# Nucleus search of a graph network's second step: the last threshold move takes its slope from the move before it, one estimate is made by one engine alone, and the sort has six rounds

## The chip, the core and the metric

The kernel runs on one core of a Trainium2 chip. A core has five engines that run their own instruction queues in order: PE (matrix multiply, with its weight loads shown as PEld), DVE (vector), ACT (scalar functions), POOL and SP; here SP only starts transfers. The metric is the time of one execution on the device in microseconds (us), as the median of several runs.

## The reference, cut to what matters

There are 4096 nodes with 256 features. A graph attention layer comes first and is not touched. The second layer does two steps of attention with a cut, each followed by a mix with the graph, and ends in a normalisation:

```python
def _top_p_attention(X, W1, W2, W3):
    q = X @ W1.T @ W2.T
    k = X @ W3.T
    probs = softmax(q @ k.T)                     # 4096 x 4096
    idx = argsort(-probs); sp = sorted probs; cs = cumsum(sp)
    keep_sorted = cs - sp < 0.9                  # the largest ones, up to 0.9 of the mass
    A = probs * mask
    return A / A.sum(-1)

R = (S + I) / row sums
for n in range(2):
    A = _top_p_attention(Xa, W1, W2, W3)
    Xf = R @ Xf
    Xa = A @ Xa
    Z = Z + Xf @ U1[n].T + Xa @ U2[n].T
h = X + Z, normalised, scaled and shifted; then added to x and normalised again
```

The costly part is to find, in each row of 4096 probabilities, the smallest one that is still kept.

## The kernel before, in words

The kernel has three stages: the graph attention up to about 930 us of the profiled span, step one of the nucleus layer to about 1800 us, step two from there to the end. The change concerns step two (`n == 1`).

**A tile.** A step works on 32 tiles of 128 rows (`RowTile`). A tile's 4096 logits come from PE in four pairs of 128x512 blocks (`logits`, L928), tile `lp`. The pool of `lp` has two buffers, so pair k+1 cannot start before ACT has copied pair k to `p` (`logits_evict`, L934). DVE finds the largest value (`top`, L945), ACT takes the exponentials (L952 and L963, two halves each). Then a threshold is found that lies a little above the cut:

- `scalars` and `scalars2` make the first threshold `t` from the row's spread.
- Three times (`estimate`, `join`, `move`; k = 0, 1, 2) the mass below `t` is summed and `t` is moved. For k = 0 DVE sums a quarter of the row (L1025, 128x1024). For k = 1 and 2 DVE sums one half of the row (128x2048) and ACT the other half by two passes, Relu and Sign (`estimate_half`, L1042 and L1045). `join` puts the halves together on DVE (L1060 to L1066), ACT takes a logarithm `y` (L1069), DVE makes the move `s` (L1077), ACT makes the new `t` (L1087) and the next goal (L1015).
- `lift` and `final`: DVE zeroes all values at or over `t` into `w` and sums the rest (128x4096).
- `tops`: the eight largest of each 128 of `w` (L938). `sort`: eight rounds of "largest eight, then strike them out" (L1117, L1119) give the 64 largest below `t`. `edge` and `inside` find in them where the cut lies; `cut` takes what is under it out of `p` (DVE L1177 strikes, POOL L1181 subtracts).
- `product`: PE transposes `p` (L1193), ACT copies the result (`at`, L1202), PE multiplies with the features (`ap`, L1211).

If a row's cut does not lie within the sorted values, a flag is set, and the whole layer is computed again by a general path at the end.

**Beside it.** The mix with the graph (`Mix`, tile `rp`, L1271) is 64 row blocks of PE work in both steps together, of which most fall into step two. Each of its eight parts (a "chunk": four blocks of rows, two matmuls each) is put between other PE work; after the last, ACT copies `rp` to `fx` (L1290), and `done` scales and splits it (DVE L1294, ACT L1296, L829, L830). From the middle of step two on, each finished block also goes through the output part (`place_out`: PE products `zp`, L1332, and two normalisations on DVE, ACT and POOL, L1343 to L1373).

**The order.** All four compute engines carry out what a plan says. Each part gets a time in units of one tile, tile i at i plus an offset of the table `T2` (L1388); the parts are sorted by these times, and the sorted order is the order of each engine's queue. The times set the order alone, not when something runs. The mixes of step two follow each other at `T2["mix"]`, 0.567 of a tile. Several tiles are under way at once: while tile i+1 gets its logits, tile i is at its last estimates and tile i-1 in its product.

In this text "p0" to "p3" are the ACT copies of the four pairs of logits, and "the sign block" is what ACT does for one half estimate: `t`, goal, Relu, Sign and two small copies of `t` (L1087, L1015, L1042, L1045, L1048, L1049). In the queue of ACT before the change, the sign block of tile i for k = 2 stands between p0 and p1 of tile i+1.

Of the kernel before, what the change touches and what calls it, by code (L numbers as in the profile page):

```python
# [16 lines left out]
AF = mybir.ActivationFunctionType  # L17
ALU = mybir.AluOpType
# [161 lines left out]
def graph_attention(  # L180
# [534 lines left out]

CHUNK = 128
TOP = 8
EST = (  # L720
    ((4.0, 0.8, 0.8), (8.0, 0.5, 1.2)),
    ((4.0, 1.0, 1.0), (8.0, 0.8, 0.8), (18.0, 0.5, 1.2)),
)
ROUNDS = (3, 8)
SUB = 4
START, SLOPE = 0.2, -2.65
ALONE = 0.04
SCALE = 2.0**11
TOL = 1e-5

# [2 lines left out]
def nucleus_layer(  # L733
# [5 lines left out]
    nc = tc.nc  # L739
    N = out.shape[0]  # L740
# [14 lines left out]
    for k, u in enumerate((U1T, U2T)):  # L755
        t = one.tile([P, STEPS, 2, D], F32, name=f"u{k}")
# [18 lines left out]
    def row(name, values):  # L775
        t = one.tile([P, len(values)], F32, name=name)
        for k, v in enumerate(values):
            nc.gpsimd.memset(t[:, k : k + 1], v)
        return t
# [2 lines left out]
    gains = [  # L782
        row(f"gains{n}", [down for _, down, _ in e] + [e[-1][2]]) for n, e in enumerate(EST)
    ]
    aims = [row(f"aims{n}", [aim for aim, _, _ in e]) for n, e in enumerate(EST)]

    xa = one.tile([P, NT, D + 1], F32, name="xa")
# [12 lines left out]
    junk_s = one.tile([P, N // 2], U8, name="junk_s")  # L800
    junk_v = one.tile([P, N // 2], U8, name="junk_v")
# [78 lines left out]
    class RowTile:  # L880
# [109 lines left out]
        def scalars2(self):  # L990
            q, z = self.q_row, all_z[:, self.at, :]
            self.gain = self.tiny("gain", len(self.est) + 1)
            nc.vector.tensor_scalar(self.gain, gains[self.n], q, None, ALU.mult)
            self.tau = self.tiny("tau")
            nc.vector.tensor_scalar(self.tau, q, SLOPE, START, ALU.mult, ALU.add)

            self.left = self.tiny("left")
            if self.n == 0:
                nc.vector.tensor_scalar(
                    self.left, self.z, TOP_P, self.zc, ALU.mult, ALU.subtract  # L1000
                )
                self.rest = self.tiny("rest")
                nc.vector.tensor_scalar(self.rest, self.zc, self.rz, -1.0, ALU.mult, ALU.mult)
                nc.vector.tensor_scalar(self.rest, self.rest, 1.0 + 1e-6, None, ALU.add)
            else:
                nc.vector.tensor_scalar(self.left, self.z, TOP_P - 1.0, None, ALU.mult)
                self.rest = small
                self.rzs = self.tiny("rzs")
                nc.vector.tensor_scalar(self.rzs, self.rz, float(SUB), None, ALU.mult)


        def set_goal(self, k):
# [14 lines left out]
            )  # L1027
            return b

        def halves(self, k):  # L1030

            return self.n and k

        def estimate_half(self, k):

            if self.halves(k):
                cols = self.p[:, N // 2 :]
                part = self.tiny("halves", 6)
                self.signs, self.gaps, self.t_half, self.t_all, self.m, self.both = (
                    part[:, i : i + 1] for i in range(6)  # L1040
                )
                nc.scalar.activation(  # L1042
                    junk_s, cols, AF.Relu, bias=self.t, scale=-1.0, accum_out=self.gaps
                )
                nc.scalar.activation(  # L1045
                    junk_s, cols, AF.Sign, bias=self.t, scale=-1.0, accum_out=self.signs
                )
                nc.scalar.activation(self.t_half, self.t, AF.Copy, scale=0.5)  # L1048
                nc.scalar.activation(self.t_all, self.t, AF.Copy, scale=float(N // 4))  # L1049

        def estimate(self, k):
            sub = SUB if self.n and k == 0 else 2 if self.halves(k) else 1
            b = self.under(junk_v, sub)
            self.b, self.sub = b, sub

        def join(self, k):
            b, sub = self.b, self.sub
            if self.halves(k):

                nc.vector.tensor_scalar(  # L1060
                    self.m, self.signs, self.t_half, self.t_all, ALU.mult, ALU.add
                )
                nc.vector.tensor_scalar(
                    self.m, self.m, self.gaps, 0.0, ALU.subtract, ALU.max
                )
                nc.vector.tensor_scalar(self.both, self.m, b, None, ALU.add)  # L1066
                b, sub = self.both, 1
            self.y = self.tiny("y")
            nc.scalar.activation(  # L1069
                self.y, b, AF.Ln, scale=self.rzs if sub > 1 else self.rz, bias=self.rest  # L1070
            )

        def move(self, k):

            last = k == len(self.est) - 1
            s = self.tiny("s")
            nc.vector.tensor_scalar(  # L1077
                s, self.y, self.goal, self.gain[:, k : k + 1], ALU.subtract, ALU.mult
            )
            if last:  # L1080
                s1, s = s, self.tiny("s2")
                nc.vector.tensor_scalar(
                    s, self.y, self.goal, self.gain[:, k + 1 : k + 2], ALU.subtract, ALU.mult
                )
                nc.vector.tensor_scalar(s, s, s1, None, ALU.min)
            self.t = self.tiny("t")
            nc.scalar.activation(self.t, s, AF.Exp, scale=-1.0, bias=self.tau)  # L1087
            if not last:
                tau = self.tiny("tau")
                nc.vector.tensor_scalar(tau, self.tau, s, None, ALU.subtract)  # L1090
                self.tau = tau
                self.set_goal(k + 1)

        def lift(self):

            f = self.tiny("f")
            nc.vector.tensor_scalar(f, self.t, self.rz, ALONE, ALU.mult, ALU.is_ge)
            t = self.tiny("tf")
            nc.vector.tensor_scalar(t, f, 10.0, self.t, ALU.mult, ALU.add)
            self.t = t  # L1100
# [277 lines left out]
    def at(time, part, *args):  # L1378
        plan.append((time, len(plan), part, args))
# [3 lines left out]
        tops=0.105, top=0.882, spread0=1.093, exp_cand=1.477, spread1=0.939, exp0=1.191,  # L1383
# [1 line left out]
        move1=1.853, lift=1.861, final=1.897, sort=1.983, edge=2.281, select=2.299, product=2.548,  # L1385
        lag=0.218, out=0.344, qt=0.253, q1=0.460, q2=0.612, space=0.125, apart=0.250, split=0.300,
    )
    T2 = dict(top=0.512, spread0=0.616, spread1=0.514, exp0=0.670, exp1=0.604, scalars=0.726, scalars2=0.793, est0=0.807, join0=0.813, move0=0.856, est1=0.884, join1=0.931, move1=1.062, est2=1.204, join2=1.220, move2=1.326, lift=1.522, final=1.619, tops=1.657, sort=1.824, edge=2.072, inside=2.085, cut=2.275, product=2.354, lag=0.090, out=0.060, qt=-0.078, q1=0.444, q2=0.541, space=0.067, apart=0.074, mix=0.567, copy=0.030)  # L1388

    def carry_out():  # L1390
        for _, _, part, args in sorted(plan, key=lambda e: e[:2]):
# [56 lines left out]
    def place_second(t, time):  # L1448

        place_queries(t, time - 1, T2)  # L1450
        for k in range(4):
            at(time + k * T2["apart"] + 0.01, t.logits, k)
            at(time + k * T2["apart"] + T2["copy"], t.logits_evict, k)
        at(time + T2["top"], t.top)
        for k in range(2):
            at(time + T2[f"spread{k}"], t.spread, k)
            at(time + T2[f"exp{k}"], t.exp, k)
        at(time + T2["scalars"], t.scalars)
        at(time + T2["scalars2"], t.scalars2)
        for k in range(len(EST[1])):  # L1460
            if k:
                at(time + T2[f"move{k - 1}"] + 0.002, t.estimate_half, k)
            at(time + T2[f"est{k}"], t.estimate, k)
            at(time + T2[f"join{k}"], t.join, k)
            at(time + T2[f"move{k}"], t.move, k)
        at(time + T2["lift"], t.lift)
        at(time + T2["final"], t.final)
        for b in range(8):
            at(time + T2["tops"], t.tops, w, b)
        for k in range(ROUNDS[1]):  # L1470
            at(time + T2["sort"] + 0.018 * k, t.sort, k)
        at(time + T2["edge"], t.edge)
        at(time + T2["inside"], t.inside)
        for k in range(4):
            at(time + T2["cut"] + 0.04 * k, t.cut, k)
        place_product(t, time + T2["product"], T2)

    def place_out(m, time):
        at(time + 0.03, m.out_load)
        at(time - 0.3, m.out_load_f)  # L1480
        at(time + 0.3, m.out_load_x)
        for k in range(4):
            at(time + 0.01 + 0.09 * k, m.out_transpose, k)
            at(time + 0.06 + 0.09 * k, m.out_product, k)
        at(time + 0.36, m.out_sum)
        at(time + 0.50, m.out_norm)
        at(time + 0.70, m.out_stats)
        at(time + 0.80, m.out_store)

# [3 lines left out]
    with tc.manual_schedule(  # L1495
# [16 lines left out]
        time = 0.0  # L1512
# [6 lines left out]
        for i, m in enumerate(mixes[1]):  # L1519
            time = max(time, i + 3.4)  # L1520
# [423 lines left out]
```

## Time and profile before

| | |
|---|---|
| median of 3 runs | 3541.23 us (3536.95 to 3541.74) |
| the profiled execution | 3550.11 us, of it 3548.3 us span |
| busy in the span | PE 91%, DVE 83%, ACT 71%, PEld 58%, POOL 17% |
| graph attention, 0 to 930 us | PE 820.5, DVE 802.7, ACT 739.7 us busy |
| step one, 930 to 1800 us | PE 848.3, DVE 634.8, ACT 654.0 us busy |
| step two, 1800 to 3549 us | PE 1556.8, DVE 1521.0, ACT 1120.1 us busy |

The tiles of step two begin (DVE L945) at 1867.0 us for the first and 3393.3 us for the last. The table of stages that the profile gives has one row per stretch of time, with each engine's busy time in it, the granted clock of PE as a share of full speed, and the DMA traffic. A view of waits says which instruction of an engine stood idle for whom, with the total, the number of times and the longest.

### The profile page before, as it was taken

To read this page: it belongs to the slowest core of one execution; us is meant where nothing else is said; L and a number is where in the kernel's file an instruction comes from. 1 tells how busy PE (TensorE), PEld (TensorE's weight loads), DVE (VectorE), ACT (ScalarE), POOL (GpSimd) and SP (SyncE) were. 2 spreads that over 40 slices of the span, in tenths; PEclk is the share of its full clock that TensorE was granted. 3 is DMA by queue.
4 is the path that set the end of the run, shared out by engine and by line. 5 is a ranking of instruction groups with operands and counts; after the bars stand their busy time and mean duration, and the time that the engine had idled before them with its cause. 6 is when DMAs were issued, how large, how long until landed. Compare 5 with 4: busy or idle time off the path is not lost. (4 is left out here: it accounts for less than half of the span.)

```text
span 3548.3 us, 56062 instructions
## 1 busy us (share of the span) xinstructions
PE 3225.7 (91%) x19538; PEld 2074.7 (58%) x19538; DVE 2958.4 (83%) x8775; ACT 2513.8 (71%) x3938; POOL 601.7 (17%) x433
## 2 busy tenths in 40 slices
PE   8998889888789999999997899999899989999987
PEld 4522222222357777777874667666667767767765
DVE  4779989999568888888516999999989999999993
ACT  4678889889578888888516776677667667667652
POOL 1101450000000000000000222222222332322331
PEclk9999999999899999999998999999899999999998
DMA  9846543232332222222235444444544444444433
GB/s 211 133 112 143 128 125 129 104 111 87 96 123 104 81 102 104 104 82 102 92 120 151 118 119 112 116 116 118 160 108 107 106 114 108 106 112 106 111 79 79
DMA packets 637302, 402.60 MB, mean 113 GB/s; under 512 B 262672, under 2 KB 588304, under 8 KB 633936
## 3 DMA queue, kind: packets, MB, share of 16 engines
q1 hardware_dynamic: 626640, 315.03, 31.3%
q10 hardware_dynamic: 1536, 67.11, 5.2%
q0 software_dynamic: 8832, 16.78, 5.1%
q8 instruction: 155, 2.54, 0.3%
q14 instruction: 139, 1.14, 0.1%
HBM read 406.03 MB, written 118.62 MB: 148 GB/s over the span
## 5 line engine op out<-in xcount | busy, mean ns | idle before, releaser
L1271 PE MATMUL rp<-low,adj 128*128 128x258 f32 x1856 | 561.2, 392 | 30.4 <-ACT fx L1290 17.7
L1271 PE MATMUL rp<-p,short 128*128 128x256 f16 x1856 | 501.4, 297 | 0.3 <-DMA short<-adj_d 0.2
L604 DVE COPY_PREDICATED other<-mask,e 128x2048 f32<-128x2048 uint8 x176 | 451.6, 2575 | 53.6 <-ACT other L589 48.1
L1211 PE MATMUL ap<-xf,at 128*128 128x257 f32 x2048 | 495.4, 387 | 0.0
L1211 PE MATMUL ap<-xa,at 128*128 128x257 f32 x2048 | 487.5, 381 | 4.0 <-ACT at L1202 3.9
L1271 PEld LDWEIGHTS rp<-low,adj 128*128 128x128 f32 x1856 | 391.6, 211 | 139.8 <-issue 84.1
L1211 PEld LDWEIGHTS ap<-xf,at 128*128 128x128 f32 x2048 | 372.4, 190 | 133.2 <-ACT t L1087 22.7
L928 PE MATMUL lp<-kT,q 64*128 64x512 f32 x1024 | 349.6, 713 | 110.5 <-ACT p L934 109.9
L634 PE MATMUL acc<-other,v 128*32 128x512 f32 x2816 | 344.7, 608 | 76.9 <-DVE other L604 65.1
L582 ACT ACTIVATE e<-src,minus_flat,factors 128x2048 f32<-128x2048 f32 x176 | 367.9, 2090 | 64.9 <-DVE other L604 31.8
L1202 ACT COPY at<-tpa 128x512 f32<-128x512 f32 x448 | 261.1, 584 | 208.5 <-PE tpa L1193 206.7
L1211 PEld LDWEIGHTS ap<-xa,at 128*128 128x128 f32 x2048 | 372.4, 191 | 49.4 <-ACT at L1202 5.8
L589 ACT ACTIVATE other<-away,minus_flat 128x2048 f32<-128x2048 f32 x176 | 350.6, 1992 | 8.0 <-PE acc L634 6.2
L1181 POOL TENSOR_TENSOR p<-p,w 128x1024 f32<-128x1024 f32 x128 | 299.8, 2365 | 312.8 <-DVE w L1177 271.5
L934 ACT COPY p<-lp 128x512 f32<-128x512 f32 x512 | 273.0, 584 | 93.3 <-PE lp L928 93.0
L1193 PE MATMUL tpa<-ident,p 128*128 128x128 f32 x2048 | 311.2, 275 | 2.2 <-POOL p L1181 2.2
L952 ACT ACTIVATE junk_s<-p,htop 128x2048 uint8<-128x2048 f32 x128 | 255.7, 1997 | 40.7 <-DVE htop L947 40.4
L1193 PEld LDWEIGHTS tpa<-ident,p 128*128 128x128 f32 x2048 | 246.0, 141 | 40.3 <-issue 3.3
L1177 DVE MATCH_REPLACE8 w<-c,w 128x128 f32<-128x128 f32 x1024 | 268.0, 276 | 0.0
L634 PEld LDWEIGHTS acc<-other,v 128*32 128x32 f32 x2816 | 81.1, 111 | 304.8 <-DVE other L604 152.8
L963 ACT ACTIVATE p<-p,ntop 128x2048 f32<-128x2048 f32 x128 | 257.8, 2014 | 0.1
L938 DVE MAX8 c<-p 128x8 f32<-128x128 f32 x1024 | 209.6, 277 | 55.0 <-ACT p L934 51.8
(259 smaller groups left out, 5451.1 us busy)
## 6 DMA issues: line engine op xcount, KB each, us to landing
adj<-adj_d SPq DMA_DIRECT2D x464, 256.0 KB
mask<-adj_d SPq DMA_DIRECT2D x164, 256.0 KB
short<-adj_d SPq DMA_DIRECT2D x232, 128.0 KB
mask<-mask_d SPq DMA_DIRECT2D x60, 256.0 KB
adj<-in_adjT SPq DMA_DIRECT2D x48, 256.0 KB
mask<-in_adjT POOLq DMA_DIRECT2D x32, 256.0 KB, 8.1
adj_d<-mask SPq DMA_DIRECT2D x32, 256.0 KB
src<-src_d SPq DMA_DIRECT2D x8, 1024.0 KB
```

Source lines behind the costliest of these rows:

```text
L582: nc.scalar.activation(self.e, self.head.src, AF.Relu, scale=self.factor(0), bias=self.factor(2))
L589: nc.scalar.activation(self.other, self.head.away, AF.Identity, bias=self.factor(2))
L604: nc.vector.copy_predicated(self.other, self.mask, self.e)
L634: nc.tensor.matmul(head.acc[k][at : at + 32, :], weights, self.e[:, b * 512 : (b + 1) * 512], tile_position=(0, at), **ends,)
L928: nc.tensor.matmul(lp, self.q[rows, :], kT[rows, at], start=True, stop=True)
L934: nc.scalar.copy(self.p[:, b * 512 : (b + 1) * 512], lp)
L1177: nc.vector.match_replace(w[:, cols], self.cand[:, c * TOP : (c + 1) * TOP], w[:, cols], 0.0)
L1181: nc.gpsimd.tensor_tensor(self.p[:, cols], self.p[:, cols], w[:, cols], ALU.subtract)
L1193: nc.tensor.transpose(tp[:, q * P : (q + 1) * P], self.p[:, (b * 4 + q) * P : (b * 4 + q + 1) * P], ident,)
L1202: nc.scalar.copy(at, tp)
L1211: nc.tensor.matmul(self.ap[:, : D + 1], at[:, q * P : (q + 1) * P], self.cur[:, j, :], start=j == 0, stop=j == NT - 1,)
L1271: nc.tensor.matmul(self.rp[:, : part.shape[1]], a, part, start=start and k == 0, stop=stop and k == len(parts) - 1,)
```

## The change

Four things change in step two, and nothing in the other stages:

1. For k = 1 DVE no longer sums its half; the half that ACT sums stands for the row (scaled by 2). For k = 2 both halves are summed as before, and ACT takes two logarithms: one of its own half, one of the whole.
2. The last move divides the step of the second move by what it changed in ACT's half, within the bounds 0.48 and 0.64, in place of two fixed factors. That is seven small DVE instructions for three. The aims of the three estimates become 16, 16, 16 (they were 4, 8, 18), and the bound at which `lift` gives up a threshold 0.025 (0.04).
3. The sort has six rounds, 48 values.
4. The table `T2` has new offsets, the mix 0.576, and three output parts stand earlier.

```diff
-    ((4.0, 1.0, 1.0), (8.0, 0.8, 0.8), (18.0, 0.5, 1.2)),
+    ((16.0, 0.9, 0.9), (16.0, 0.9, 0.9), (16.0, 0.48, 0.64)),
-ROUNDS = (3, 8)
+ROUNDS = (3, 6)
-ALONE = 0.04
+ALONE = (0.04, 0.025)
...
         def estimate(self, k):
-            sub = SUB if self.n and k == 0 else 2 if self.halves(k) else 1
-            b = self.under(junk_v, sub)
+            self.b = self.under(junk_v, (4, None, 2)[k] if self.n else 1)
...
         def join(self, k):
+            if self.n and k:
                 nc.vector.tensor_scalar(
                     self.m, self.signs, self.t_half, self.t_all, ALU.mult, ALU.add
...
+                self.y_before, self.y_half = self.y, self.log_of(self.m, 1)
+                if k == 1:
+                    self.y = self.y_half
+                    return
                 nc.vector.tensor_scalar(self.both, self.m, b, None, ALU.add)
...
         def move(self, k):
+            if last and self.n:
+                nc.vector.tensor_scalar(less, self.y_before, self.y_half, 1.0 / CAREFUL[0], ALU.subtract, ALU.mult)
+                nc.vector.tensor_scalar(square, less, less, 1e-12, ALU.mult, ALU.add)
+                nc.vector.reciprocal(square, square)
+                nc.vector.tensor_scalar(more, self.moved, less, square, ALU.mult, ALU.mult)
+                nc.vector.tensor_scalar(more, more, gain, self.gain[:, k + 1 : k + 2], ALU.max, ALU.min)
+                nc.vector.tensor_scalar(error, self.y, self.goal, more, ALU.subtract, ALU.mult)
+                nc.vector.tensor_scalar(s, error, CAREFUL[1] / CAREFUL[0], error, ALU.mult, ALU.min)
...
-    T2 = dict(top=0.512, ... est1=0.884, join1=0.931, move1=1.062, est2=1.204, join2=1.220, move2=1.326, lift=1.522, ... sort=1.824, edge=2.072, inside=2.085, cut=2.275, product=2.354, ... mix=0.567, copy=0.030)
+    T2 = dict(top=0.481, ... join1=0.945, move1=1.068, est2=1.200, join2=1.232, move2=1.395, lift=1.497, ... sort=1.827, edge=2.032, inside=2.121, cut=2.230, product=2.354, ... mix=0.576, copy=0.042)
...
-        at(time + 0.50, m.out_norm)
-        at(time + 0.70, m.out_stats)
-        at(time + 0.80, m.out_store)
+        at(time + 0.46, m.out_norm)
+        at(time + 0.62, m.out_stats)
+        at(time + 0.70, m.out_store)
```

More of the change, by code (lines that the diff above doesn't have):

```diff
@@ L721 @@
     ((4.0, 0.8, 0.8), (8.0, 0.5, 1.2)),
-    ((4.0, 1.0, 1.0), (8.0, 0.8, 0.8), (18.0, 0.5, 1.2)),
+    ((16.0, 0.9, 0.9), (16.0, 0.9, 0.9), (16.0, 0.48, 0.64)),
 )
-ROUNDS = (3, 8)
-SUB = 4
+CAREFUL = (0.8, 1.2)
+ROUNDS = (3, 6)
+SHARES = (4.0, 2.0)
 START, SLOPE = 0.2, -2.65
-ALONE = 0.04
+ALONE = (0.04, 0.025)
 SCALE = 2.0**11
@@ L784, in nucleus_layer @@
     ]
+    shares = row("shares", SHARES)
     aims = [row(f"aims{n}", [aim for aim, _, _ in e]) for n, e in enumerate(EST)]
@@ L1007, in scalars2 @@
                 self.rest = small
-                self.rzs = self.tiny("rzs")
-                nc.vector.tensor_scalar(self.rzs, self.rz, float(SUB), None, ALU.mult)
+                self.rzs = self.tiny("rzs", 2)
+                nc.vector.tensor_scalar(self.rzs, shares, self.rz, None, ALU.mult)
         def set_goal(self, k):
@@ L1028, in under, with estimate_half, log_of @@
             return b
[L1030 to L1049, printed above, removed]
-        def estimate(self, k):
-            sub = SUB if self.n and k == 0 else 2 if self.halves(k) else 1
-            b = self.under(junk_v, sub)
-            self.b, self.sub = b, sub
+        def estimate_half(self):
+            cols = self.p[:, N // 2 :]
+            part = self.tiny("halves", 6)
+            self.signs, self.gaps, self.t_half, self.t_all, self.m, self.both = (
+                part[:, i : i + 1] for i in range(6)
+            )
+            nc.scalar.activation(
+                junk_s, cols, AF.Relu, bias=self.t, scale=-1.0, accum_out=self.gaps
+            )
+            nc.scalar.activation(
+                junk_s, cols, AF.Sign, bias=self.t, scale=-1.0, accum_out=self.signs
+            )
+            nc.scalar.activation(self.t_half, self.t, AF.Copy, scale=0.5)
+            nc.scalar.activation(self.t_all, self.t, AF.Copy, scale=float(N // 4))
+        def estimate(self, k):
+            self.b = self.under(junk_v, (4, None, 2)[k] if self.n else 1)
+        def log_of(self, b, share=None):
+            y = self.tiny("y")
+            scale = self.rz if share is None else self.rzs[:, share : share + 1]
+            nc.scalar.activation(y, b, AF.Ln, scale=scale, bias=self.rest)
+            return y
         def join(self, k):
-            b, sub = self.b, self.sub
-            if self.halves(k):
+            b, share = self.b, 0 if self.n and k == 0 else None
+            if self.n and k:
                 nc.vector.tensor_scalar(
@@ L1065, in join @@
                 )
+                self.y_before, self.y_half = self.y, self.log_of(self.m, 1)
+                if k == 1:
+                    self.y = self.y_half
+                    return
                 nc.vector.tensor_scalar(self.both, self.m, b, None, ALU.add)
[L1067 to L1071, printed above, removed]
+                b = self.both
@@ L1073, in move @@
+            self.y = self.log_of(b, share)
         def move(self, k):
             last = k == len(self.est) - 1
+            gain = self.gain[:, k : k + 1]
             s = self.tiny("s")
[L1077 to L1081, printed above, removed]
+            if last and self.n:
+                part = self.tiny("slope", 4)
+                less, square, more, error = (part[:, i : i + 1] for i in range(4))
@@ L1082, in move @@
                 nc.vector.tensor_scalar(
-                    s, self.y, self.goal, self.gain[:, k + 1 : k + 2], ALU.subtract, ALU.mult
+                    less, self.y_before, self.y_half, 1.0 / CAREFUL[0], ALU.subtract, ALU.mult
                 )
-                nc.vector.tensor_scalar(s, s, s1, None, ALU.min)
+                nc.vector.tensor_scalar(square, less, less, 1e-12, ALU.mult, ALU.add)
+                nc.vector.reciprocal(square, square)
+                nc.vector.tensor_scalar(more, self.moved, less, square, ALU.mult, ALU.mult)
@@ new lines, in move @@
+                nc.vector.tensor_scalar(
+                    more, more, gain, self.gain[:, k + 1 : k + 2], ALU.max, ALU.min
+                )
+                nc.vector.tensor_scalar(
+                    error, self.y, self.goal, more, ALU.subtract, ALU.mult
+                )
+                nc.vector.tensor_scalar(
+                    s, error, CAREFUL[1] / CAREFUL[0], error, ALU.mult, ALU.min
+                )
+            else:
+                nc.vector.tensor_scalar(s, self.y, self.goal, gain, ALU.subtract, ALU.mult)
+                self.moved = s
+                if last:
+                    s1, s = s, self.tiny("s2")
+                    nc.vector.tensor_scalar(
+                        s, self.y, self.goal, self.gain[:, k + 1 : k + 2], ALU.subtract, ALU.mult
+                    )
+                    nc.vector.tensor_scalar(s, s, s1, None, ALU.min)
@@ L1096, in lift @@
             f = self.tiny("f")
-            nc.vector.tensor_scalar(f, self.t, self.rz, ALONE, ALU.mult, ALU.is_ge)
+            nc.vector.tensor_scalar(f, self.t, self.rz, ALONE[self.n], ALU.mult, ALU.is_ge)
             t = self.tiny("tf")
@@ L1387, in nucleus_layer @@
     )
-    T2 = dict(top=0.512, spread0=0.616, spread1=0.514, exp0=0.670, exp1=0.604, scalars=0.726, scalars2=0.793, est0=0.807, join0=0.813, move0=0.856, est1=0.884, join1=0.931, move1=1.062, est2=1.204, join2=1.220, move2=1.326, lift=1.522, final=1.619, tops=1.657, sort=1.824, edge=2.072, inside=2.085, cut=2.275, product=2.354, lag=0.090, out=0.060, qt=-0.078, q1=0.444, q2=0.541, space=0.067, apart=0.074, mix=0.567, copy=0.030)
+    T2 = dict(top=0.481, spread0=0.650, spread1=0.518, exp0=0.653, exp1=0.593, scalars=0.728, scalars2=0.769, est0=0.800, join0=0.820, move0=0.835, join1=0.945, move1=1.068, est2=1.200, join2=1.232, move2=1.395, lift=1.497, final=1.643, tops=1.647, sort=1.827, edge=2.032, inside=2.121, cut=2.230, product=2.354, lag=0.090, out=0.060, qt=-0.077, q1=0.461, q2=0.489, space=0.067, apart=0.074, mix=0.576, copy=0.042)
     def carry_out():
@@ L1461, in place_second @@
             if k:
-                at(time + T2[f"move{k - 1}"] + 0.002, t.estimate_half, k)
-            at(time + T2[f"est{k}"], t.estimate, k)
+                at(time + T2[f"move{k - 1}"] + 0.002, t.estimate_half)
+            if k != 1:
+                at(time + T2[f"est{k}"], t.estimate, k)
             at(time + T2[f"join{k}"], t.join, k)
```

## The prediction

> **What bounds the kernel now.** The page comes first, then the table of stages for step two alone, since nothing else changes. One stretch has only mixes beside the search (11 tiles), the other has the output part too (13 tiles):
>
> ```profile
> core 0: us, PE busy (x) PEld busy (x) DVE busy (x) ACT busy (x) POOL busy (x), PEclk, DMA share, GB/s
> 2001.10:2508.90 507.80, 465.23 (x2602) 345.95 (x2603) 482.25 (x1859) 356.33 (x651) 124.69 (x75) 0.93 0.46 117
> 2661.00:3344.60 683.60, 630.19 (x3625) 484.28 (x3624) 643.56 (x2494) 470.70 (x952) 201.89 (x134) 0.97 0.43 109
> ```
>
> A tile takes 46.2 us in the first stretch and 52.6 us in the second. DVE is busy 95% and 94% of it, PE 92% in both. DVE looks like the bound. The waits of 2000 to 2500 us, by engine, say whether it is the only one:
>
> ```profile
> PE lp L928 <- ACT p L934: 34.9, 16, 4.3
> PE rp L1271 <- ACT fx L1290: 7.4, 5, 4.0
> ```
>
> ```profile
> DVE all_z L977 <- ACT p L963: 7.8, 5, 2.6
> DVE halves L1060 <- ACT halves L1049: 2.9, 3, 1.6
> DVE s L1077 <- ACT y L1069: 0.7, 1, 0.7
> ```
>
> DVE's named waits are 11.4 us in eleven tiles, 1.0 a tile; about 1.3 us more are unnamed gaps between its some 170 instructions a tile. PE's waits are 42.3 us, nearly all its idle time in that stretch (507.8 less 465.2). So PE stands still only for ACT's copies, 3.8 us a tile. The order of time shows where (PE and ACT, one tile):
>
> ```profile
> 2167.51 1.13 PE L928 MATMUL lp<-kT,q 64*128 64x512 f32 x4
> 2170.25 1.61 PE L928 MATMUL lp<-kT,q 64*128 64x512 f32 x4 [0.44 <-ACT p L934]
> 2176.12 1.79 PE L928 MATMUL lp<-kT,q 64*128 64x512 f32 x4 [3.08 <-ACT p L934]
> ```
>
> ```profile
> 2169.64 1.05 ACT L934 COPY p<-lp 128x512 f32<-128x512 f32 x2
> 2170.58 0.30 ACT L1087 ACTIVATE t<-s,tau 128x1 f32<-128x1 f32 x1
> 2173.32 2.00 ACT L1045 ACTIVATE junk_s<-p,t 128x2048 uint8<-128x2048 f32 x1
> 2175.51 1.04 ACT L934 COPY p<-lp 128x512 f32<-128x512 f32 x2
> ```
>
> PE finishes pair 0, ACT copies it (p0), then ACT runs the whole sign block (2170.58 to 2175.51, 4.9 us) before p1, and pair 2 waits for p1's buffer. PE has only two mix chunks and pair 1 to put into that time, some 3.3 us. Hence a stall of 3 to 4 us in nearly each tile. Its price is larger than itself:
>
> ```profile
> 2168.40:2175.88 7.48, 4.20 (x22) 2.40 (x20) 7.10 (x23) 7.41 (x15) 0.67 (x1) 1.00 0.80 206
> 2175.88:2184.00 8.12, 7.88 (x25) 4.26 (x25) 8.02 (x58) 3.39 (x8) 4.67 (x2) 0.59 0.23 50
> ```
>
> After the stall PE runs at a granted clock of 0.59 over 8.1 us, that is, some 6.8 us at half speed, 3.4 us of PE work lost.
>
> So there are two loops of nearly the same length. **PE's loop:** from the end of pair 0 to the start of pair 2, 7.95 us in the mean of tiles 3 to 14 (6.54 the shortest); from there to the end of the next tile's pair 0, 37.97 us, nearly without a wait. Sum 45.9 us. **DVE's loop:** 43.8 us busy, 1.3 of gaps, 1.0 of waits: 46.1 us. The change shortens the second by much and the first by little.
>
> **The change part by part.** The rows, from 2300 to 3100 us (16 tiles):
>
> ```profile
> L1025 DVE SCALAR_TENSOR_TENSOR junk_v<-p,t 128x2048 uint8<-128x2048 f32 x32 | 75.0, 2344 | 2.4 <-ACT t L1087 2.4
> L1117 DVE MAX8 s<-left 128x8 f32<-128x256 f32 x111 | 47.0, 423 | 1.0
> L1119 DVE MATCH_REPLACE8 left<-s,left 128x256 f32<-128x256 f32 x96 | 39.3, 409 | 0.0
> L1077 DVE TENSOR_SCALAR s<-y,goal,gain 128x1 f32<-128x1 f32 x48 | 12.7, 264 | 0.8 <-ACT y L1069 0.6
> ```
>
> *DVE, per tile.* The half sum of k = 1 goes: 2.34 and 0.08 for its accumulator. Its joining addition (L1066, 0.21) goes. Two rounds of sorting go, each 0.42 + 0.41 + 0.09 for the load of the values: 1.85. `edge` works on 48 in place of 64: its scan takes 0.28 at 64 and 0.92 at 256 wide, 3.3 ns an element, 0.05 for 16; four others at some 1 ns, 0.07; together 0.12. The last move loses 0.26 + 0.26 + 0.21 = 0.74 and gains seven instructions that the trace does not have: by nearest rows (0.21 with one column as operand, 0.26 with two, 0.15 a reciprocal), 3 x 0.21 + 3 x 0.26 + 0.15 = 1.56; between 1.1 (all at 0.15) and 1.9. Net 2.34 + 0.08 + 0.21 + 1.85 + 0.12 + 0.74 - 1.56 = 3.8 us a tile, 121 us over 32.
>
> *ACT, per tile.* One more logarithm, 0.39 (L1069). It stands between p2 and p3, where in the trace ACT has time: it is idle 30% in these stretches. Nothing on the path; if uncovered, 12 us in all.
>
> *A new wait.* Between the move of k = 0 and its join, DVE had tau (0.21), four rounds (3.7) and the half sum (2.43): 6.3 us, over ACT's 4.9 for the sign block and its start. In the changed order it has tau, four rounds and one more MAX8: 0.21 + 3.70 + 0.42 = 4.3 us. DVE will wait 0.8 us or more at L1060, more where ACT waits for PE ahead of the block (in one tile 1.31 us for `tpa`). Behind it in DVE's queue stand the edge, the cut and the next tile's maximum. Bounds 0.5 and 2.5, I take 1.1. DVE's loop becomes 43.8 - 3.8 + 1.3 + 1.0 + 1.1 = 43.4 us.
>
> *PE's loop.* The order of PE and ACT around the stall stays: p0, sign block, p1, and one chunk between pairs. What goes is lateness: p0 came 0 to 1.7 us after pair 0 was ready (2168.64 to 2169.64 above), because ACT was behind DVE, whose maximum started 2 to 3 us after p3 was done. With DVE ahead, I put pair 0 to pair 2 at 6.9 us, near the shortest. The mix costs PE 19.1 us each (515.5 us for 27 in the same window); at 0.576 a tile holds 1.736 of them, not 1.764: 0.5 us less. 6.9 + 37.97 - 0.5 = 44.4 us. PE's loop is then the longer one.
>
> A rule speaks for more. The Trainium skill, "Perfetto Trace Analysis", section Identifying the Most-Contended Engine, says the engine with the highest occupancy is the one to optimise first; that is DVE, and taken alone it would pay out all 121 us, less the new wait. The waits of PE speak against it: 92% busy, and all of the rest tied to ACT in a loop of 45.9 us. I follow the loop. Another rule bears on the stall: "TensorE: Matmul & The Clock Gate", section HAM oscillation, warns of idle gaps over some 3.4 us. The trace has half speed after 3.08 already. My 6.9 less 3.3 leaves 3.6 us, so the half speed stays; if the stall fell clear of it, another 3.4 us a tile would come.
>
> *Output part.* In most tiles with outputs a scaling of `h` (L1354, 0.60) stood in ACT's queue between p0 and the block; with the earlier offsets it is gone from there. The earlier store also gives the single buffer of `h` more time: DVE waited 13.6 us in all for `out_y`. Pair 0 to pair 2 was 8.5 us here, the rest 44.3. I take 1.2 off the first (0.6 and lateness) and 0.5 off the second: 1.7 a tile. POOL's work is unchanged in amount, and moved away from its subtractions.
>
> *The end.* The longer mix step pushes 27 x 0.5 = 14 us of PE work behind tile 28, where PE had room (81.7 of 98.4 us busy at 3344 to 3443). It is hidden there, but then PE is full and DVE's saving in the last two tiles, 6 us, shrinks to 2. The last tile alone gains two rounds less what the new last move costs: 1.5.
>
> *Sum:* tiles 3 to 15, 13 x 1.6 = 21; tiles 16 to 29, 14 x 1.7 = 24; tiles 1 and 2, where p0 waits up to 7 us for DVE, 2 x 3 = 6; the last two, 2; the end, 1.5. Together 54 us. The profiled execution of 3550.1 us would become 3496; it lies 9 us over the median, and the same 54 us below the median give 3487. Differences under 0.2%, 7 us, could not be told from none.
>
> **The rivals.**
>
> *DVE's saving comes through (chance 0.15).* If lateness sits in all of PE's loop and the stall also drops under the half-speed point, tiles follow DVE's 43.4: 2.7 a tile, 85 us, and up to 120 without the new wait. For it: DVE's 95%. Against: PE's named waits.
>
> *The waits eat most (0.12).* If the join wait is 2.5 us and PE's loop keeps its lateness, 7 to 30 us remain.
>
> *Slower (0.07): the join of k = 1.* The place is L1060 behind the sign block; its price is whatever ACT's queue puts in front. DVE now has 4.3 us of cover. At a wait of more than 3.8 us the tile is longer than before, and each further us costs 32. That needs ACT to start the block 3 us late, as when `at` waits for `tpa` on PE; 1.31 us was seen, so it is unlikely. At 5 us: 38 us slower.
>
> *A missed row (0.03).* Only 48 values are sorted. I worked the new threshold rule through on the reference's inputs in float32: the farthest cut is the 45th value under the threshold. It is not far from 48[...]. One missed row adds the graph attention again (930 us) and a general search, milliseconds.
>
> **How the numbers follow.** The likeliest case, 30 to 80 us off, has 0.60, with 54 its middle: 3487. Full pass-through 0.15, small gain 0.12, no change 0.03, slower 0.10. The range leaves out the top of the full gain (over 100 us) and gains under 16 with what is slower: 3440 to 3525. Faster 0.87, same 0.03, slower 0.10.
>
> **What would show it.** DVE busy in step two falls by some 120 us, from 1521. A new wait of DVE at the join for ACT's `halves`, some 30 us in all. PE's wait for `p` stays at 3 us a tile and half speed stays after it; PE becomes the busiest, at 95% or more, DVE under 92%. Tiles at 44.4 and 50.9 us. If the stall of PE disappears, or tiles fall under 43.5, my loop was wrong; if DVE stays at 95%, the wait or the added instructions were mis-sized.

## The result and the profile after

The changed kernel takes 3508.70 us (median of 6 runs, 3506.38 to 3513.61), the kernel before in the same session 3539.38 us (6 runs, 3532.73 to 3545.73). The ratio is 0.9916, with a 95% interval of 0.9902 to 0.9930: 31 us faster, where 54 had been forecast; that lies at the lower edge of the likeliest case, 30 to 80. Line numbers of step two differ from those before by up to 23; the names, such as `lp` or `halves`, are the same.

The table of stages of the profile after, for the same 11 and 13 tiles as in the prediction, and then from tile 30 to the end:

```profile
1995.90:2492.50 496.60, 456.95 (x2594) 341.34 (x2594) 449.16 (x1802) 359.34 (x660) 120.74 (x75) 0.93 0.47 118
2632.40:3299.60 667.20, 629.48 (x3601) 483.51 (x3599) 604.06 (x2428) 476.00 (x964) 220.90 (x134) 0.96 0.44 111
3299.60:3505.50 205.90, 173.01 (x968) 138.26 (x966) 137.51 (x575) 95.72 (x203) 52.93 (x40) 0.90 0.37 94
```

A tile takes 45.1 us without outputs (46.2 before) and 51.3 with them (52.6). DVE, the third engine of the row after PE and PEld, fell from 95% to 90% busy; PE stayed at 92% in the first stretch and went from 92% to 94% in the second. The clock is 0.93 and 0.96, as good as unchanged. The waits of PE and of DVE in the first stretch:

```profile
PE lp L931 <- ACT p L937: 32.6, 11, 4.3
PE rp L1294 <- ACT fx L1313: 6.5, 5, 3.9
```

```profile
DVE halves L1062 <- ACT halves L1047: 16.8, 11, 2.6
DVE all_z L980 <- ACT p L966: 6.4, 8, 2.3
```

PE's wait for `p` is as it was (it was 34.9 us in 500), and DVE has the new wait at the join of k = 1, 1.5 us in each of eleven tiles. The order of time of one tile shows the reason (PE, then ACT; rows between are left out):

```profile
2204.31 1.13 PE L931 MATMUL lp<-kT,q 64*128 64x512 f32 x4
2212.69 1.96 PE L931 MATMUL lp<-kT,q 64*128 64x512 f32 x3 [3.60 <-ACT p L937]
```

```profile
2205.53 1.06 ACT L937 COPY p<-lp 128x512 f32<-128x512 f32 x2
2207.16 0.30 ACT L1110 ACTIVATE t<-s,tau 128x1 f32<-128x1 f32 x1
2212.08 1.05 ACT L937 COPY p<-lp 128x512 f32<-128x512 f32 x2
```

Pair 0 ends at 2205.44, and p0 starts 0.09 us later. In the mean of tiles 3 to 14 p0 was 1.1 us late before and is 0.25 us late now. The block (2207.16 to 2212.08, 4.9 us) and the stall of 3.6 us stand as they were. The chain that ended last, by engine, before and after (shares of the span; both chains reach back only over the last third of it):

```profile
DVE 12%; PE 11%; ACT 4%; issue 2%; DMA 1%; POOL 0%; SPq 0%; POOLq 0%; DVEq 0%; ACTq 0%
```

```profile
PE 18%; ACT 4%; DVE 4%; issue 2%; POOL 0%; DMA 0%; POOLq 0%; DVEq 0%; ACTq 0%
```

In this last third DVE's part fell from 12% to 4% of the span, and PE's rose from 11% to 18%.

From the starts of the tiles in both traces, the profiled executions (3550.11 and 3507.40 us) differ so: up to tile 3, 5 us less; tiles 3 to 15, 19 less; tiles 16 to 29, 21 less; from tile 30 to the end of the span, 2.5 more (205.9 against 203.4).

### The profile page after: what moved, and what is told of

Its sections match the earlier page's. It is cut to its first block, busy times and chain, and to the rows that moved or that the text cites. A ratio compares the mean times of both kernels' runs of the same rounds, so it can differ in the third digit from the quotient of the medians.

```text
span 3505.5 us, 55976 instructions
## 1 busy us (share of the span) xinstructions
PE 3219.6 (92%) x19538; PEld 2073.3 (59%) x19538; DVE 2862.1 (82%) x8615; ACT 2526.9 (72%) x3970; POOL 610.9 (17%) x435
```

## The experiments

Each kernel was timed beside the kernel before on the same chip. "Faster" and "slower" in us below compare medians of different sessions. The kernel before had medians of 3539 to 3548 us in these sessions, so such differences are good to some 9 us; the ratios carry their intervals, 5 to 9 us to either side.

| run | ratio to the kernel before | interval |
|---|---|---|
| the change | 0.9916 | 0.9902 to 0.9930 |
| 1, changed, eight rounds again | 0.9916 | 0.9897 to 0.9935 |
| 2, changed, DVE's half sum again | 0.9894 | 0.9876 to 0.9912 |
| 3, changed, mix spacing of before | 0.9919 | 0.9901 to 0.9937 |
| 4, changed, logits later | 0.9923 | 0.9908 to 0.9939 |
| 5, before, new order | 1.0032 | 1.0018 to 1.0045 |
| 6, changed, old order | 0.9956 | 0.9939 to 0.9973 |
| 7, changed, Sign pass twice | 1.0119 | 1.0099 to 1.0138 |
| 8, changed, half the mix | 0.9720 | 0.9700 to 0.9741 |
| 9, changed, block split | 0.9754 | 0.9737 to 0.9771 |
| 10, changed, block shorter | 0.9811 | 0.9792 to 0.9830 |
| 11, changed, split and shorter | 0.9768 | 0.9745 to 0.9790 |
| 12, before, block split | 0.9925 | 0.9904 to 0.9947 |

**Does DVE's saved work matter?** Two runs put parts of it back, with the rest of the change in place.

```diff
-ROUNDS = (3, 6)
+ROUNDS = (3, 8)
```

> The changed kernel with eight rounds of sorting again: DVE works 1.85 + 0.1 us more in each of 32 tiles, 62 us in all, and nothing else is different. Theory (PE's loop through ACT's sign block sets the tile, DVE has slack): DVE's tile was 40.8 busy of 44.9 us, with 1.5 us of it a wait at the join, so most of the 1.95 us fits into slack: 0 to 12 us slower than the changed kernel, about 3508 to 3521. Rival (DVE is the bound, as its 91 to 94% busy says): 50 to 62 us slower, 3560 or more, worse than the kernel before.

```diff
-            self.b = self.under(junk_v, (4, None, 2)[k] if self.n else 1)
+            b = self.under(junk_v, (4, 2, 2)[k] if self.n else 1)
+            if not (self.n and k == 1):
+                self.b = b
...
-            if k != 1:
-                at(time + T2[f"est{k}"], t.estimate, k)
+            at(time + (T2[f"est{k}"] if k != 1 else 0.900), t.estimate, k)
```

> The changed kernel with DVE's half sum for k = 1 done again, its result unused: 2.43 us of DVE work a tile, 78 us in all, put between the move of k = 0 and the join where DVE waits for ACT's sign block (16.8 us in some eleven tiles, 1.5 a tile). Theory: 1.5 us of it go into the wait and the rest into DVE's slack: 0 to 20 us slower than the changed kernel. Rival (DVE is the bound): 30 to 78 us slower, 30 if only the wait is filled.

Eight rounds: 3515.61 us, ratio 0.9916 as with the change. The half sum done again: 3502.63 us, and no slower either. DVE was busy 54 us longer in the one and 66 in the other (2915.6 and 2927.6 against 2862.1 us in the whole run), and neither cost anything that can be told from the spread. In the second run DVE's wait at the join went from 16.8 us (in 480) to 0.8:

```profile
DVE halves L1064 <- ACT halves L1047: 0.8, 2, 0.4
```

The wait was part of the room into which the work fitted. DVE alone as the bound is refuted. That the second run is a little below the change (0.9894 against 0.9916) is within the overlap of the intervals.

**The mix's spacing.**

```diff
-... mix=0.576, copy=0.042)
+... mix=0.567, copy=0.042)
```

> The changed kernel with the mixes 0.567 of a tile apart as before. Theory: each of some 27 tiles has 0.5 us more PE work (13 us), and the end, where PE did 13.5 us more than before and took 4 us more instead of 3 less, becomes shorter by 5 to 13 us: between 5 us faster and 8 us slower, no clear difference. Rival (PE's work in the tiles is not on the path): faster by the whole of the end, 5 to 13 us.

3514.51 us, no difference. In its trace, tile 30 to the end takes 202.1 us, against 205.9 with 0.576, and tiles 3 to 29 take 7 us longer. What the wider spacing saves in the tiles it gives back at the end, as far as one trace of each can tell.

**Is the stall the bound?** First, by moving the logits.

```diff
-            at(time + k * T2["apart"] + 0.01, t.logits, k)
-            at(time + k * T2["apart"] + T2["copy"], t.logits_evict, k)
+            at(time + k * T2["apart"] + 0.01 + 0.14, t.logits, k)
+            at(time + k * T2["apart"] + T2["copy"] + 0.14, t.logits_evict, k)
```

> The changed kernel with the four logits pairs and their copies 0.14 of a tile later in the order, so that ACT's sign block for k = 2 stands ahead of p0 and PE has two more mix chunks (2 us) to do while it runs. Amounts of work are the same. Theory (the stall of PE at pair 2 and the half speed after it set the tile): the stall shrinks from some 3.2 to 2.5 us or less and half speed is met less often: 1 to 3 us a tile, 25 to 80 us faster than the changed kernel, 3430 to 3485, until DVE's 43.4 us a tile binds. Rival (DVE is the bound, or the stall is only where slack shows): no gain, or slower because the maximum of the next tile starts later.

3517.15 us: no gain, a miss. The stall did shrink (PE waited 18.0 us for `p` from 2000 to 2480 us, against 29.5), but the tiles without outputs kept 44.8 us. The next maximum now stood waiting for the last copy of the logits, 14.8 us on `ntop` in that window, where there had been none:

```profile
PE lp L931 <- ACT p L937: 18.0, 10, 3.4
DVE ntop L948 <- ACT p L937: 14.8, 11, 1.7
```

Read from the order of the kernel, there is beside PE's loop a chain of nearly the same length: last logits, maximum, exponentials, first estimate, sign block, logarithm, p0, second sign block, cut, next maximum.

**Order or arithmetic?** Two runs cross them: the old arithmetic with the new table and output offsets, and the new with the old ones.

```diff
-    T2 = dict(top=0.512, ... mix=0.567, copy=0.030)
+    T2 = dict(top=0.481, ... est1=0.900, join1=0.945, ... mix=0.576, copy=0.042)
...
-        at(time + 0.50, m.out_norm)
+        at(time + 0.46, m.out_norm)
```

> The kernel before with the changed order table and output offsets (its half sum for k = 1 put at 0.900), all of its arithmetic kept. It splits the change in two. If the gain comes from the order alone: 3505 to 3515, like the changed kernel. If it comes from less DVE work: no gain, 3535 to 3550. Theory after the first four runs (DVE has 2 to 2.5 us a tile to spare in the changed kernel, and 4 us come back here): about half, 3515 to 3530.

```diff
-    T2 = dict(top=0.481, ... mix=0.576, copy=0.042)
+    T2 = dict(top=0.512, ... mix=0.567, copy=0.030)
...
-        at(time + 0.46, m.out_norm)
+        at(time + 0.50, m.out_norm)
```

> The changed arithmetic in the old order table, with the old output offsets. If the gain comes from the order alone: 3535 to 3545. If it comes from less DVE work alone: 3505 to 3515. Theory: PE's loop loses its lateness by DVE's lead in this order too, but the outputs and the mix keep their old places: 3515 to 3530.

3552.89 and 3525.44 us. The arithmetic is worth 0.44% in the old order (0.9956) and 1.16% in the new one (from 1.0032 to 0.9916); the new order is worth 0.40% with the new arithmetic and costs 0.32% with the old. The first expectation was a miss: I had put the new order at half the gain, and alone it loses. In that run DVE waits 13.5 us for the exponentials from 2000 to 2480 us (7.8 in 500 us of the kernel before); why the new table lengthens that part with the old arithmetic is open. Returning one part of DVE's work costs nothing (runs 1 and 2), returning all costs 1.16%. In tiles 3 to 15 DVE is busy 40.8 us a tile with the change, 42.9 in run 2 at the same tile time, and 44.0 in run 5, where the tile is 2 us longer: DVE has some 2 us a tile to spare, and what exceeds it is paid.

**The price of the sign block.** One run lengthens it by a pass whose result is not used:

```diff
...
+            if k == 2:
+                nc.scalar.activation(junk_s, cols, AF.Sign, bias=self.t, scale=-1.0)
```

> The changed kernel with ACT's Sign pass for k = 2 done twice, between p0 and p1: 2.0 us more of ACT in each of 32 tiles, 64 us in all, on an engine that is 72% busy; DVE and PE have the same work. Theory (the tile is a loop through this block, whether by PE's pair 2 or by the join on DVE): nearly all of it shows, 50 to 65 us slower than the changed kernel, 3558 to 3573. Rival (an engine's amount of work is the bound): 0 to 10 us, since ACT has 28% idle.

3580.51 us, 72 us slower than the change (50 to 65 expected) for 64 us of ACT work, on an engine with 28% idle. So the block lies on the path of the tiles, at its full price or a little more.

**The price of PE's work.** Here half of the mix's row blocks are left out.

```diff
-            for jj in range(JC):
+            for jj in range(0, JC, 2 if self.in_parts else 1):
```

> The changed kernel with every other row block of the mixes in step two left out (both matmuls; all loads stay): about half of 14 us of PE work a tile, 7 us, while ACT and DVE have the same work. If PE's loop alone sets the tile, it falls until DVE's busy time and its waits bind, near 43 us: 3430 to 3460. If the chain from the maximum over ACT and DVE back to the next maximum is as long as PE's loop (the late logits pointed to that, 44.8 us a tile with the stall nearly halved), stretches without output stay near 44 us and only those with output fall: 3460 to 3490. Rival (DVE or ACT alone sets the time): no gain.

3443.41 us, 65 us faster. In tiles 3 to 15 PE's busy time fell from 41.1 to 36.5 us, but the tile only from 44.9 to 43.4 (tiles 16 to 29: 51.4 to 49.3). PE is then busy 85% of the first stretch and DVE 94%:

```profile
2000.00:2480.00 480.00, 405.63 (x1981) 288.29 (x1980) 449.40 (x1807) 358.42 (x663) 122.22 (x74) 0.88 0.50 125
```

So PE's loop was the longest, by 1.5 to 2 us, and right below it lies another bound, as the first case of the expectation had it. Whether that is DVE's own time (40.7 us busy, with its gaps and waits 43.4) or the chain seen in run 4, this run does not tell.

**Opening the loop.** The order was then changed in one place: p1 between the two passes of the block.

```diff
             nc.scalar.activation(
                 junk_s, cols, AF.Relu, bias=self.t, scale=-1.0, accum_out=self.gaps
             )
+
+        def estimate_sign(self):
+            cols = self.cols
             nc.scalar.activation(
                 junk_s, cols, AF.Sign, bias=self.t, scale=-1.0, accum_out=self.signs
             )
...
+                at(time + (T2[f"move{k - 1}"] + 0.003, T2["apart"] + T2["copy"] + 1.002)[k - 1], t.estimate_sign)
```

> The changed kernel with ACT's sign block for k = 2 opened: p1 stands between the Relu and the Sign pass, order alone, all work the same. PE's pair 2 waits 2.2 us less, but pair 3 then waits for the rest of the block, so PE has two stalls of some 1.3 us in place of one of 3.2, and the half speed after the long one (3.4 us a tile) should go; the join of k = 2 comes 1.05 us later. Theory (PE's loop 44.9 us a tile, the chain over DVE and ACT 43.4 as the halved mix showed): PE's loop falls to some 40, the chain becomes 44.4: 0.5 us a tile without output, 1 to 2 with output, 15 to 40 us faster than the changed kernel, 3470 to 3495. If only the total of work counts: no change. If the later join matters at once: up to 30 us slower.

3458.64 us, ratio 0.9754: 50 us faster than the change by the medians (57 by the ratios), 86 faster than the kernel before, and with run 11 the best of all runs that do the whole work. It is more than the 15 to 40 us expected: the chain over DVE and ACT was to grow to 44.4 us by the later join, and the tile fell to 43.4. The order of time of a tile in it (PE, then ACT):

```profile
2194.63 1.61 PE L931 MATMUL lp<-kT,q 64*128 64x512 f32 x4 [1.29 <-ACT p L937]
2198.96 1.61 PE L931 MATMUL lp<-kT,q 64*128 64x512 f32 x4 [1.55 <-ACT p L937]
```

```profile
2192.03 1.99 ACT L1041 ACTIVATE junk_s<-p,t 128x2048 uint8<-128x2048 f32 x1
2194.01 1.05 ACT L937 COPY p<-lp 128x512 f32<-128x512 f32 x2
2194.96 2.00 ACT L1048 ACTIVATE junk_s<-p,t 128x2048 uint8<-128x2048 f32 x1
```

Two short stalls stand where one of 3.6 us was. The stages from 2000 to 2480 us, of the change and of this run:

```profile
2000.00:2480.00 480.00, 443.44 (x2526) 332.29 (x2524) 432.92 (x1726) 350.77 (x642) 111.38 (x70) 0.94 0.47 118
```

```profile
2000.00:2480.00 480.00, 445.66 (x2593) 337.56 (x2592) 449.77 (x1810) 355.71 (x661) 122.34 (x74) 0.98 0.50 125
```

The work of a tile is the same: the granted clock rose from 0.94 to 0.98, DVE from 90% to 94% busy. A tile takes 43.4 us without outputs and 50.1 with them. From tile 3 to tile 29 the clock stood at half speed for 44 us in place of 140, and PE's busy time for a tile fell by 1.0 to 1.1 us (41.1 to 40.0 without outputs). So most of the 1.5 us of such a tile shows as a faster PE, the rest as less idle time.

**A shorter block, alone and with the split.**

```diff
-SHARES = (4.0, 2.0)
+SHARES = (4.0, 2.2857142857142856)
...
-            cols = self.p[:, N // 2 :]
+            cols = self.p[:, 2304 :]
...
-            self.b = self.under(junk_v, (4, None, 2)[k] if self.n else 1)
+            self.b = self.under(junk_v, (N // 4, None, 2304)[k] if self.n else None)
```

> The changed kernel with ACT's part of the row 1792 columns, not 2048, for k = 1 and 2, and DVE's 2304: each of ACT's four passes is 0.25 us shorter, the sign block 0.5; DVE works 0.27 us more. Theory (the block lies in every loop, at the price of one to one, as the doubled pass showed with 2.2 us a tile for 2.0): 0.5 us a tile or a little more (the chain has two blocks), 14 to 28 us faster than the changed kernel, 3480 to 3495. Rival (amounts of work on DVE count): 9 us slower.

> Both: p1 between Relu and Sign, and ACT's part 1792 columns. Theory: PE's loop is out of the way, and the chain loses two times 0.5 us: 43.4 us a tile without output, 30 to 65 us faster than the changed kernel, 3445 to 3480. If the two gains are one and the same: as the better of the two.

Alone: 3474.95 us, 34 us faster than the change, more than the 14 to 28 foretold: 0.8 to 0.9 us a tile for 0.5 off each of two blocks. Both: 3459.81 us, no better than the split alone, the second case of the expectation. With both, DVE is busy 455.27 of 480 us, 95%, as in the kernel before: it is full again. That this is what stops the second gain is argued from the number, not tried.

**The split on the kernel before.** The same order edit, in the old table and with the old arithmetic:

```diff
+                at(time + (T2[f"move{k - 1}"] + 0.003, T2["apart"] + T2["copy"] + 1.002)[k - 1], t.estimate_sign, k)
```

> The kernel before with p1 between the Relu and the Sign pass of k = 2, order alone. On the changed kernel this took the stall apart and was worth 57 us. Here DVE still works 43.9 us a tile in the stretch without output and 49.6 with it. Theory (before, DVE's loop of 46.1 us and PE's of 45.9 are both full): PE's loop falls but DVE's stays, so little is gained without output (0 to 0.5 us a tile) and up to 1.5 with output: 0 to 25 us faster than before, 3518 to 3543; the changed arithmetic is then worth 60 to 85 us in the opened order, where it was worth 16 in the old order. Rival (PE's stall alone set the time before as well): 50 to 60 us faster, 3482 to 3492, and the arithmetic is worth 25 to 35.

3520.07 us against 3547.97, ratio 0.9925, at the edge of the theory's span and far from the rival's. In the opened order the change is worth 61 us (3520.07 to 3458.64); with the block closed, 31. PE's stall took half of it. Seen the other way, the opened block alone gives 28 us and the change alone 31, and both together give 86, more than their sum: each alone runs into the loop that the other shortens.

## Why the prediction was right or wrong

**Two loops, DVE's and PE's, of equal length: right.** Runs 1, 2 and 12 show both: with the change DVE's work is free to come back in part; before it, opening PE's stall alone gives only 0.75%. The prediction did not have the bound right below PE's loop, 43.4 us, that runs 8 and 9 met. Its sign of a PE at 95% or more did not come either: PE was busy 92% and 94%.

**DVE's saving of 3.8 us a tile, 121 in all: too large.** Busy time fell by 3.1 to 3.2 us a tile, 96 in all (1521.0 to 1425.1). The seven instructions came as sized (0.16 to 0.27 each, 1.6 together). The rows' durations, which I added up, overlap in the trace: the half sum's accumulator read of 0.08 starts before the sum has ended. Added up over step two, the durations of all DVE instructions fell by 117 us (1802.6 to 1685.7), near the 121 forecast; the overlap makes the difference to 96. The forecast of the tile was spared because it rests on PE's loop. The margin was thin: with 3.1 saved and a wait of 1.5 the prediction's own sum gives 44.5 us for DVE's loop, no longer less than the 44.4 of PE's.

**The new wait of 1.1 us: right in place, 1.5 measured.** It is harmless, because it lies in DVE's spare time; run 2 fills it at no cost. The slower rival needed 3.8 us there.

**PE's loop at 44.4 us by the end of lateness: right in kind, 0.6 us short.** Lateness went to 0.1 us in most tiles, and pair 0 to pair 2 to 7.1 us in the mean of tiles 3 to 14 (7.95 before, 6.9 forecast). But the rest of the loop, from which 0.5 us was taken for the wider mix spacing, stayed at 37.9 us (37.97 before; 37.9 in run 3 with the old spacing). Tiles 3 to 15 gained 19 us where 21 were forecast, tiles 16 to 29 gained 21 where 24 were, the first ones 5 for 6. In the output part the wait for `out_y` went as forecast, from 13.6 us to none; DVE waited for `zp` in its place, 24.5 us from 2630 to 3300 us.

**The stall and half speed stay: right without outputs.** With outputs the stall at pair 2 fell from 2.7 to 1.8 us a tile, and the clock stayed at 0.96 to 0.97. The prediction set the gap of some 3.4 us of the Trainium skill ("TensorE: Matmul & The Clock Gate", HAM oscillation) against the row of 3.08 us and took no gain from it. Here the clock fell after shorter gaps still (last section). Run 9 shows what stall and half speed were worth together: gaps of 1.3 and 1.6 us, a clock of 0.98, 50 us.

**The end: wrong.** The step was "It is hidden there, but then PE is full and DVE's saving in the last two tiles, 6 us, shrinks to 2." PE did 13.5 us more from tile 30 on (173.0 against 81.66 and 77.87, 159.5 us, before), and it was not hidden: the end is 2.5 us longer instead of 3.5 shorter. The rows of before:

```profile
3344.60:3443.00 98.40, 81.66 (x440) 62.70 (x439) 95.02 (x370) 65.99 (x128) 27.82 (x19) 0.91 0.31 81
3443.00:3549.00 106.00, 77.87 (x442) 62.36 (x440) 46.27 (x209) 24.85 (x61) 25.56 (x20) 0.89 0.32 82
```

Run 3 shows it the other way round: with the old spacing PE does 160.6 us there, and the end is 3.8 us shorter than with the change.

**The base: wrong.** "the same 54 us below the median" took the profiled execution's 9 us over the median as common to both kernels. The execution after lies at its median (3507.40 and 3508.70). Between the profiled executions the gain is 43 us, between the medians 31; these 12 us are about half of the miss of 23; the shortfalls in the tiles and at the end are the other half. What made that one execution of before longer is not shown; single executions of that kernel ranged from 3525 to 3558 us in these sessions. The gains by stage above are those of two single executions.

**Full pass-through: refuted.** The Trainium skill ("Perfetto Trace Analysis", Identifying the Most-Contended Engine) would have one work on the engine of highest occupancy, in these stretches DVE. Taking 96 us of work off it paid 31; on the changed kernel a copy moved on ACT, the third busiest, paid 50. On the kernel before, the same move paid 28, so neither engine alone was the one to work on.

## What to carry to other kernels

Before an engine's work is cut, look at where the other engines' waits end: if one idles in each round for the same copy, its loop may be as long as the busy engine's, and the saving ends there. A long pair of passes between two copies that free a buffer, in the queue of one engine, can be opened at no cost in work; here shorter stalls of PE also kept its clock up. Count work that is pushed to the end of a kernel as on the path until a trace shows that it is hidden. And add up busy time, not the durations of rows, when they overlap.

## What the runs showed of the hardware

In tiles 3 to 29 the granted clock of PE fell to half speed within 5 us of 24 of the 28 gaps of 2 us and more before the change, and of 25 of 26 after it (the shortest was 2.1 us). Most of these drops lasted 3.4 or 6.8 us. After gaps of 1 to 2 us it fell in 7 of 31 cases (run 9, for 3.4 us each; four of them from 1990 to 2300 us). A stall of 3.1 us followed by 6.8 us at half speed loses 3.1 and 3.4 us of PE work, by this estimate about twice its length.

In the traces the durations of neighbouring DVE instructions overlap: in step two of the kernel before they add up to 1802.6 us, and the engine was busy 1521.0.
